# Two adapter layers in Winograd form: where the second down phase keeps its first inputs and its first bias

## The chip, the cores and the metric

The kernel runs on one core of a Trainium2 chip. The metric is the device time of one execution in microseconds. TensorE multiplies, ScalarE, VectorE and GpSimd do the elementwise work, and SyncE issues nearly all DMA transfers. Everything is float32.

## What is computed

There are two layers with the same form. Each of 128 samples (128 rows of 1024 numbers) has a role, one of three, and each role has weights of its own. A layer goes down to 512 numbers, through a Gelu, up to 1024, adds its input, and normalises:

```python
def _L0_cond_ref(role, hidden_states, W_down, b_down, W_up, b_up, gamma, beta):
    h = jnp.einsum('bsh,bhk->bsk', hidden_states, W_down[role]) + b_down[role][:, None, :]
    h = jax.nn.gelu(h, approximate=False)
    u = jnp.einsum('bsk,bkh->bsh', h, W_up[role]) + b_up[role][:, None, :]
    y = hidden_states + u
    mean = jnp.mean(y, axis=-1, keepdims=True)
    var = jnp.mean(jnp.square(y - mean), axis=-1, keepdims=True)
    yn = (y - mean) * jax.lax.rsqrt(var + LN_EPS)
    return yn * gamma[role][:, None, :] + beta[role][:, None, :]
...
    x = _L0_cond_ref(itok_B_1_2, x, L0_cond_W_down, L0_cond_b_down, L0_cond_W_up, L0_cond_b_up, L0_cond_gamma, L0_cond_beta)
    x = _L1_cond_ref(itok_B_1_2, x, L1_cond_W_down, L1_cond_b_down, L1_cond_W_up, L1_cond_b_up, L1_cond_ln_w, L1_cond_ln_b)
```

## The kernel before

**Pairs and places.** On the chip the kernel sorts the samples by role and forms 63 pairs of two samples of one role, and one left-over pair whose samples may differ. The roles are put in order of frequency; a role's position in that order is its *place*, 0 to 2. The first 21 pairs (`NFIRST`) are surely of place 0, so they need only place 0 of the weights and the biases. For the other pairs the place is read into a register.

**Phases.** The work is four phases: down and up of layer 0, down and up of layer 1. Each runs over all 64 pairs in one `sequence`, in which the left-over pair stands in the middle; so the last up pairs of a phase have the numbers 60, 61 and 62. Between the phases the results go through DRAM: `hd` holds what a down phase gives, `mid` what the up phase of layer 0 gives.

**One pair.** A pair is multiplied in Strassen-Winograd form: seven products of quarter size (`item_products`, s1 to s7 at L444 to L472), with four sums of the input quarters made by GpSimd (`winograd_sums`, L401 to L404) and four sums of weight quarters made beforehand. The products gather in three kinds of PSUM banks, b, a and e. Banks b and e begin with a copy of the bias by ScalarE (`seeded`, L428), the *seed*; a product can't begin before its seed. Between two products into the same bank the bank is read: in a down pair by ScalarE (L549, L557) or VectorE (L553), in an up pair by VectorE (L618, L627).

A `Down` pair loads x in eight transfers of 128 KB (`quartered`, L387), four for each sample; VectorE turns each sample with one block transpose (L525, the *turn*); then GpSimd's sums and the products follow. It ends with Gelus on ScalarE (L554, L557) and a store of h to `hd` (L562). An `Up` pair loads h and x (L584, L590), turns h (L596), and ends with the norm: ScalarE takes mean and squares (L689 to L694), GpSimd the inverse root (L695), VectorE scales (L698), and the last factor and beta come from ScalarE and GpSimd for one sample (L705, L706) and from VectorE for the other (L708). Then the result is stored to `mid` (L710).

**Buffers.** The tag q has four buffers of 128 x 1024. The two x of a down pair lie in it (`xqd`), and so do the two outputs of an up pair (`ou`), from L693 to their store. In the up phase q holds outputs alone; near its end it holds x of the first down pairs too. A buffer is given out in the order of the requests and is taken only when its last user is done. The tag t has three buffers, for x of an up pair or the turned x of a down pair.

**Weights.** `wall` holds eight slots; a weight block is one slot with three places of 1024 columns each. Seven blocks, named as in `ORDER`, serve a phase, and the eighth slot is free for the next phase's first block, B11. The others are loaded into the slots of the finished phase as its last products end (L813): place 0 first, places 1 and 2 over the next pairs, block by block. So the blocks of the coming phase have two unused places for some time.

**Order.** The order is written out by hand. A pair has a `base` time, in slots, 7 slots to a pair, and each step is put at a time relative to it with `at(time, step)`; the heap `events` runs the steps in order of time, and L849 to L860 keep that order on each engine. SyncE's queue is in order as well: an issue that waits holds all behind it. Eight semaphores serve the DMAs in turn, so that a transfer is issued only when the one eight before it has landed.

**Around the change.** For the first three down pairs of layer 1, `go` (which turns both samples, starts the sums and plans the products) stands at base - 7.2 (L768), the loads of x at base - 11.9 and - 11.8 (L756). The biases of that phase are loaded at L790 to L800: place 0 into table 0 just after the last up pair has begun, places 1 and 2 some pairs later, and all three once more into table 2 in the middle of the phase, since the next up phase needs table 0. The bias' right half has its left half subtracted by VectorE (L133). The first down pair has its first seed at base - 0.6 (L744) and the others at base - 4.

Of the kernel before, what the change touches and what calls it, by code (L numbers as in the profile page):

```python
# [10 lines left out]
F32 = mybir.dt.float32  # L11
I32 = mybir.dt.int32
AF = mybir.ActivationFunctionType
ALU = mybir.AluOpType
ENG = mybir.EngineType
# [4 lines left out]
P = 128  # L20
SQ = 32
NQ = P // SQ
# [4 lines left out]
def kernel(  # L27
# [57 lines left out]
    def flat(tag, bufs, name, size=2048):  # L85
        return work.tile([P, size], F32, tag=tag, name=name, bufs=bufs)
# [416 lines left out]
    class Down:  # L503
# [5 lines left out]
            self.tag = f"d{layer}_{n}"  # L509

        def load(self):
            self.xq = [
                flat("q", 4, f"xq{self.tag}_{s}", H).rearrange("p (a c) -> p a c", a=NQ)
                for s in range(2)
            ]
            self.srcs = x_of(self.layer, self.n, ENG.SP)
            quartered(self.xq[0:1], self.srcs[0:1])

        def load_rest(self):
            quartered(self.xq[1:2], self.srcs[1:2])  # L520

        def prepare(self):
            self.a = flat("t", 3, "xT" + self.tag).rearrange("p (s j c) -> p s j c", s=2, c=P)
            for s in range(2):
                nc.vector.transpose(  # L525
                    self.a[:, s].rearrange("p j (t a) -> p j a t", t=SQ),
                    self.xq[s].rearrange("p a (i j) -> p j a i", i=SQ),
                )
                if s == 0 and self.early:
                    first_sum("T1", 0)  # L530
            self.sums = None
            if self.n < NPAIR:
                self.sums = flat("s", 3, "S" + self.tag, 1792)[:, 0:1536].rearrange(
                    "p (m j c) -> p m j c", m=3, c=P
                )
                winograd_sums(self.sums, self.a, nc.vector if self.early else nc.gpsimd)
            set_places(self, [ENG.PE, ENG.Activation])
# [185 lines left out]
    def at(time, step):  # L723
        heapq.heappush(events, (time, next(count_), step))
# [7 lines left out]
    for k, ph in enumerate(phases):  # L732
        for m, n in enumerate(sequence):
            base = SLOTS * (k * NI + m)
            box = {}
            kind = Up if ph.up else Down

            def load(box=box, ph=ph, n=n, kind=kind, m=m):
                item = box["item"] = kind(ph, n)
                item.m = m  # L740
                item.early = ph is phases[0] and m == 0
                item.last = ph is phases[-1] and m == NI - 1
                if ph is phases[2] and m == 0:
                    item.SEED = -0.6  # L744
                if m == left_over_at + 1:
                    item.SEED = -1.65
                item.load()


            if ph.up:  # L750
                first, rest = (-16 if m < 3 else -11.5), -7
            elif k == 0:
                first = {0: -30, 1: -19, 2: -19, 3: -17.4}.get(m, -19)
                rest = -27 if m == 0 else first + 0.05
            else:
                first, rest = -11.9, -11.8  # L756
            at(base + first, load)
            at(base + rest, lambda box=box: box["item"].load_rest())

            def go(box=box, base=base):  # L760
                item = box["item"]
                item.prepare()
                for time, step in item.products() + item.finish():
                    at(base + time, step)


            prepare = {1: 3.5 - base, 2: 8.6 - base}.get(m, kind.PREPARE) if k == 0 else kind.PREPARE
            at(base + (-7.2 if ph is phases[2] and m < 3 else prepare), go)  # L768
        if k + 1 < len(phases):

            nxt = phases[k + 1]
            later_places = lambda time, load: [
                at(base + time + SLOTS * 2 * i, lambda k_=k_: load([k_])) for i, k_ in enumerate(range(1, R))
            ]
            place_0, others = slice(0, 1), slice(1, R)
            if nxt.up:
                at(base - 2 * SLOTS, lambda nxt=nxt: nxt.new_bias(0))
                at(base - 2 * SLOTS, lambda nxt=nxt: nxt.load_bias([0]))
                at(base - 2 * SLOTS + 3, lambda nxt=nxt: nxt.subtract(place_0))
                at(base - 2 * SLOTS + 3, nxt.set_bias)  # L780
                at(base - 2 * SLOTS, lambda nxt=nxt: nxt.load_gamma([0]))
                at(base + 2 * SLOTS - 1, lambda nxt=nxt: nxt.load_beta([0]))
                later_places(6 * SLOTS - 1, nxt.load_gamma)
                later_places(7 * SLOTS - 1, nxt.load_beta)
                later_places(10 * SLOTS - 1, lambda p, nxt=nxt: nxt.load_bias(p))
                at(base + 14 * SLOTS - 1.9, lambda nxt=nxt: nxt.subtract(others))
            else:


                at(base + 1.6, lambda nxt=nxt: nxt.new_bias(0))  # L790
                at(base + 1.6, lambda nxt=nxt: nxt.load_bias([0]))
                at(base + 4.2, lambda nxt=nxt: nxt.subtract(place_0))
                at(base + 4.2, nxt.set_bias)
                later_places(5 * SLOTS - 0.6, lambda p, nxt=nxt: nxt.load_bias(p))
                at(base + 10 * SLOTS - 1.9, lambda nxt=nxt: nxt.subtract(others))
                half = base + SLOTS * NI // 2
                at(half, lambda nxt=nxt: nxt.new_bias(2))
                at(half, lambda nxt=nxt: nxt.load_bias())
                at(half + SLOTS, lambda nxt=nxt: nxt.subtract())
                at(half + SLOTS, nxt.set_bias)  # L800

            if k == 0:
                places = [(7, -SLOTS), (5, 4), (4, 6), (0, 8), (1, 8), (2, 10), (3, 10)]
                spare = 6
            else:
                slots = [spare] + [ph.weights[name].slot for name in ORDER]
                places = [(slot, 2 * i - 2) for i, slot in enumerate(slots[:-1])]
                places[0], spare = (slots[0], -SLOTS), slots[-1]
            for name, (slot, free) in zip(ORDER, places):
                nxt.weights[name] = block = Block(slot)  # L810

                def load_part(k, to=block, src=scratch[nxt.layer, nxt.up][name]):
                    nc.sync.dma_start(to.v[:, k], src[:, k])  # L813


                at(base + free + 0.75, lambda f=load_part: f(0))
                for k_ in range(1, R):
                    later_on = SLOTS * (1 + ORDER.index(name)) + 3.5 * k_
                    at(base + later_on + 0.75, lambda f=load_part, k_=k_: f(k_))
# [70 lines left out]
```

## Time and profile before

| | |
|---|---|
| median of 3 runs | 3151.09 us (3149.3 to 3152.04) |
| the profiled execution | 3151.07 us |
| its span, first to last instruction | 3149.3 us |
| TensorE matmul busy | 3112.8 us, 99% of the span |
| VectorE | 1976.1 us, 63% |
| GpSimd | 1793.0 us, 57% |
| ScalarE | 1201.7 us, 38% |
| mean granted TensorE clock | 0.996 |
| DMA | 642.74 MB, mean 204 GB/s |

All times inside the profile count from the first instruction of the one execution that was profiled. A row of a timeline gives start, duration, engine, line, operation, what is written and read, how many instructions are merged, and in brackets how long the engine stood idle before it and what ended that. "SPq" rows are issues of transfers by SyncE. Names are the program's, without numbers: `xqd` and `xTd` are x of a down pair as loaded and as turned, `Sd` its sums; `xu`, `hTu`, `ou` are x, turned h and output of an up pair; `bu`, `au`, `eu`, `bd`, `ad`, `ed` are the PSUM banks of up and down pairs. An up product is recorded as four matmuls of 128x512 and a down product as eight of 128x256. The hand-over from the up phase of layer 0 to the down phase of layer 1 lies between 1550 and 1615 us.

### The profile page before, as it was taken

How to read it: one execution, taken by the hardware profiler on the slowest of the kernel's cores; microseconds unless marked ns; L12 is line 12 of the kernel's file. 1: busy time of each engine (PE TensorE's matmuls, PEld its weight loads, DVE VectorE, ACT ScalarE, POOL GpSimd, SP SyncE). 2: the span in 40 equal slices, each digit the busy share in tenths (PEclk: the TensorE clock that was granted, in tenths of full speed). 3: DMA queues.
4: the chain of work that ended last, by engine and by line, in shares of the span. 5: the costliest groups of instructions: out<-in, count | busy, mean ns of one | idle time of the engine just before them, and what ended most of it. 6: DMA issues, size and time to landing. Idle time of an engine off the chain costs nothing. (4 is left out here: it accounts for less than half of the span.)

```text
span 3149.3 us, 42330 instructions
## 1 busy us (share of the span) xinstructions
PE 3112.8 (99%) x10806; PEld 2056.5 (65%) x10806; DVE 1976.1 (63%) x2795; ACT 1201.7 (38%) x2814; POOL 1793.0 (57%) x1396
## 2 busy tenths in 40 slices
PE   8999999999999999999999999999999999999998
PEld 6888888888544444444478888888884444444443
DVE  5555454544678777877754444444437777777777
ACT  1222222222355545454432222222224545554554
POOL 3454444454577767777654443343436777677776
PEclk9999999999999999999999999999999999999999
DMA  7878888886886666666696555555568766666665
GB/s 189 209 208 215 208 209 205 217 210 191 284 288 214 225 213 221 215 219 220 220 252 163 129 134 138 131 129 133 130 180 294 265 217 218 219 215 223 214 226 173
DMA packets 430454, 642.74 MB, mean 204 GB/s; under 512 B 36113, under 2 KB 305938, under 8 KB 429074
## 3 DMA queue, kind: packets, MB, share of 16 engines
q1 hardware_dynamic: 429746, 638.47, 68.9%
q8 instruction: 102, 1.67, 0.2%
q10 hardware_dynamic: 480, 1.57, 0.2%
q14 instruction: 126, 1.03, 0.1%
HBM read 405.54 MB, written 234.36 MB: 203 GB/s over the span
## 5 line engine op out<-in xcount | busy, mean ns | idle before, releaser
L410 PE MATMUL bu<-wall,hTu 128*128 (+1 forms) x2048 | 924.1, 593 | 6.1 <-DVE xu L618 5.5
L525 DVE STREAM_TRANSPOSE xTd<-xqd 128x1024 f32<-128x1024 f32 x256 | 518.2, 2088 | 354.4 <-PE bd L410 275.1
L410 PEld LDWEIGHTS bu<-wall,hTu 128*128 128x128 f32 x2048 | 389.9, 190 | 495.8 <-issue 458.7
L401 POOL TENSOR_TENSOR Sd<-xTd 128x512 f32<-128x512 f32 x125 | 161.0, 1288 | 799.9 <-DVE xTd L525 799.9
L695 POOL TENSOR_TENSOR varu<-varu,mhalf 128x1 f32<-128x1 f32 x254 | 334.9, 1319 | 394.5 <-ACT varu L694 394.5
L410 PE MATMUL bd<-wall,xTd 128*128 (+1 forms) x2080 | 492.2, 380 | 4.0 <-ACT bd L428 4.0
L410 PE MATMUL eu<-wall,hTu 128*128 (+1 forms) x1040 | 488.0, 592 | 0.0
L410 PE MATMUL bd<-wall,Sd 128*128 (+1 forms) x2016 | 476.3, 379 | 0.8 <-ACT hd L549 0.8
L698 DVE SCALAR_TENSOR_TENSOR ou<-xu,meanu,tables 128x1024 f32<-128x1024 f32 x254 | 326.3, 1285 | 224.8 <-ACT ou L693 224.5
L410 PEld LDWEIGHTS bd<-wall,xTd 128*128 128x128 f32 x2080 | 396.2, 191 | 60.1 <-ACT bd L428 4.8
L410 PEld LDWEIGHTS bd<-wall,Sd 128*128 128x128 f32 x2016 | 383.0, 190 | 54.5 <-issue 2.6
L554 ACT ACTIVATE hd<-hd 128x256 f32<-128x256 f32 x382 | 158.8, 416 | 533.5 <-DVE hd L553 533.4
L410 PEld LDWEIGHTS eu<-wall,hTu 128*128 128x128 f32 x1040 | 197.6, 190 | 247.5 <-issue 224.8
L689 ACT ACTIVATE partu<-statu 128x2 f32<-128x2 f32 x254 | 51.6, 203 | 732.4 <-DVE xu L627 732.4
L706 POOL TENSOR_TENSOR ou<-ou,tables 128x1024 f32<-128x1024 f32 x127 | 299.4, 2357 | 0.0
L693 ACT ACTIVATE ou<-xu,meanu 128x1024 f32<-128x1024 f32 x254 | 291.7, 1148 | 13.5 <-DMA mid<-ou 4.9
L410 PE MATMUL ed<-wall,xTd 128*128 (+1 forms) x1072 | 254.6, 381 | 3.0 <-DVE xTd L402 3.0
L401 POOL TENSOR_TENSOR hTu<-hTu 128x256 f32<-128x256 f32 x126 | 203.2, 1613 | 65.9 <-DVE hTu L596 51.7
L410 PE MATMUL ad<-wall,xTd 128*128 (+1 forms) x1008 | 238.2, 379 | 0.0
L410 PE MATMUL ed<-wall,Sd 128*128 (+1 forms) x1008 | 238.1, 379 | 0.0
L410 PE MATMUL au<-wall,hTu 128*128 (+1 forms) x504 | 236.8, 592 | 0.0
L410 PEld LDWEIGHTS ed<-wall,xTd 128*128 128x128 f32 x1072 | 204.5, 191 | 31.9 <-issue 3.6
(110 smaller groups left out, 3329.5 us busy)
## 6 DMA issues: line engine op xcount, KB each, us to landing
xqd<-in_x_dram SPq DMA_DIRECT2D x512, 128.0 KB, 3.3
hd<-hd SPq DMA_DIRECT2D x256, 256.0 KB, 2.4
xu<-in_x_dram SPq DMA_DIRECT2D x128, 512.0 KB, 4.8
mid<-ou SPq DMA_DIRECT2D x128, 512.0 KB, 6.0
xqd<-mid SPq DMA_DIRECT2D x512, 128.0 KB, 3.9
xu<-mid SPq DMA_DIRECT2D x128, 512.0 KB, 5.8
out_dram<-ou SPq DMA_DIRECT2D x126, 512.0 KB, 5.7
hqu<-hd SPq DMA_DIRECT2D x244, 256.0 KB, 6.4
```

What stands on the lines that cost most here:

```text
L401: engine.tensor_tensor(dst[:, 1], a11, a21, ALU.subtract)
L410: nc.tensor.matmul(ps[:, 0:cols], a[:, j], w.rhs(r, j, cols), start=start and j == 0, stop=j == n - 1, skip_group_check=True,)
L525: nc.vector.transpose(self.a[:, s].rearrange("p j (t a) -> p j a t", t=SQ), self.xq[s].rearrange("p a (i j) -> p j a i", i=SQ),)
L554: nc.scalar.activation(y, y, AF.Gelu)
L689: nc.scalar.mul(part, self.stat[:, s], -1.0 / H)
L693: nc.scalar.activation(box["o"], self.x[:, s], AF.Square, bias=m, accum_out=v)
L695: nc.gpsimd.tensor_tensor(v, v, mhalf[:, 0:1], ALU.pow)
L698: nc.vector.scalar_tensor_tensor(box["o"], self.x[:, s], box["m"][:, 0:1], row(self.ph.gamma), ALU.add, ALU.mult)
L706: nc.gpsimd.tensor_tensor(o, o, row(self.ph.beta), ALU.add)
```

## The change

Four things are changed, all of them at that hand-over.

The x of the first three down pairs of layer 1 isn't loaded into q. It goes into places 1 and 2 of the weight blocks B11, B21 and T2 of the coming phase, which aren't loaded yet. The load for the first of these pairs stands at base - 15 in place of - 11.9.

For these three pairs the two turns are separate steps: the first sample's at base - 7.2, the second's with the sums at base - 5.

The first bias (place 0) has a tile of its own, `first_bias`, loaded four pairs before the last up pair and subtracted one pair later; the first down pair's seed stands at base - 4 as the others'. It serves until the twelfth down pair.

All three rows are loaded into table 2 as the eighth, ninth and tenth down pair begin, and used after their subtraction 1.9 slots ahead of the twelfth. The loads of places 1 and 2 into table 0, and those in the middle of the phase, are gone.

```diff
@@ class Down
         def load(self):
-            self.xq = [
-                flat("q", 4, f"xq{self.tag}_{s}", H).rearrange("p (a c) -> p a c", a=NQ)
-                for s in range(2)
-            ]
+            if self.among_weights:
+                block = self.ph.weights[ORDER[self.m]].v
+                self.xq = [block[:, 1 + s] for s in range(2)]
+            else:
+                self.xq = [flat("q", 4, f"xq{self.tag}_{s}", H) for s in range(2)]
+            self.xq = [t.rearrange("p (a c) -> p a c", a=NQ) for t in self.xq]
...
+        def turn(self, s):
+            nc.vector.transpose(
+                self.a[:, s].rearrange("p j (t a) -> p j a t", t=SQ),
+                self.xq[s].rearrange("p a (i j) -> p j a i", i=SQ),
+            )
+
+        def begin_turns(self):
+            self.a = flat("t", 3, "xT" + self.tag).rearrange("p (s j c) -> p s j c", s=2, c=P)
+            self.turn(0)
+
         def prepare(self):
-            self.a = flat("t", 3, "xT" + self.tag).rearrange("p (s j c) -> p s j c", s=2, c=P)
-            for s in range(2):
-                nc.vector.transpose(
-                    self.a[:, s].rearrange("p j (t a) -> p j a t", t=SQ),
-                    self.xq[s].rearrange("p a (i j) -> p j a i", i=SQ),
-                )
-                if s == 0 and self.early:
-                    first_sum("T1", 0)
+            if not self.among_weights:
+                self.begin_turns()
+            if self.early:
+                first_sum("T1", 0)
+            self.turn(1)
@@ the pairs' steps
-                if ph is phases[2] and m == 0:
-                    item.SEED = -0.6
+                item.among_weights = ph is phases[2] and m < 3
...
-                first, rest = -11.9, -11.8
+                first = -15 if m == 0 else -11.9
+                rest = first + 0.1
...
-            at(base + (-7.2 if ph is phases[2] and m < 3 else prepare), go)
+            if ph is phases[2] and m < 3:
+                at(base - 7.2, lambda box=box: box["item"].begin_turns())
+                prepare = -5
+            at(base + prepare, go)
@@ the biases of the second down phase
-                at(base + 1.6, lambda nxt=nxt: nxt.new_bias(0))
-                at(base + 1.6, lambda nxt=nxt: nxt.load_bias([0]))
-                at(base + 4.2, lambda nxt=nxt: nxt.subtract(place_0))
-                at(base + 4.2, nxt.set_bias)
-                later_places(5 * SLOTS - 0.6, lambda p, nxt=nxt: nxt.load_bias(p))
-                at(base + 10 * SLOTS - 1.9, lambda nxt=nxt: nxt.subtract(others))
-                half = base + SLOTS * NI // 2
-                at(half, lambda nxt=nxt: nxt.new_bias(2))
-                at(half, lambda nxt=nxt: nxt.load_bias())
-                at(half + SLOTS, lambda nxt=nxt: nxt.subtract())
-                at(half + SLOTS, nxt.set_bias)
+                def first_bias(nxt=nxt):
+                    nxt.bias = row = const.tile([P, 1, K], F32, name="first_bias")
+                    r = reg(role_of, 0, [ENG.SP], R - 1)
+                    nc.sync.dma_start(row[:, 0], nxt.vectors[0][ds(r, 1), :].to_broadcast((P, K)))
+
+                def subtract_first(nxt=nxt):
+                    left, right = nxt.bias[:, :, 0 : K // 2], nxt.bias[:, :, K // 2 :]
+                    nc.vector.tensor_tensor(right, right, left, ALU.subtract)
+
+                at(base - 4 * SLOTS + 0.6, first_bias)
+                at(base - 3 * SLOTS + 0.6, subtract_first)
+                at(base + 8 * SLOTS - 0.6, lambda nxt=nxt: nxt.new_bias(2))
+                for k_ in range(R):
+                    at(base + (8 + k_) * SLOTS - 0.6, lambda k_=k_, nxt=nxt: nxt.load_bias([k_]))
+                at(base + 12 * SLOTS - 1.9, lambda nxt=nxt: nxt.subtract())
+                at(base + 12 * SLOTS - 1.9, nxt.set_bias)
```

Here `base` in the last part is that of the last up pair.

## The prediction

> **What bounds the kernel now.** I read the page first: TensorE is busy for 99% of the span, at the full clock in all 40 slices, so nearly all of the time is a gapless run of matmuls and a change can gain only where that run is broken. Next I asked who TensorE waits for, in the stretch where the up phase of layer 0 hands over to the down phase of layer 1:
>
> ```profile
> PE bu L410 <- DVE xu L618: 5.5, 1, 5.5
> PE bd L410 <- ACT bd L428: 4.0, 1, 4.0
> PE bd L410 <- ACT hd L549: 0.8, 1, 0.8
> ```
>
> Columns: total us, times, longest. Three waits. The timeline of TensorE shows what they cost (start, us, what):
>
> ```profile
> 1559.49 1.88 PE L410 MATMUL au<-wall,hTu 128*128 x4
> 1561.20 1.88 PE L410 MATMUL eu<-wall,hTu 128*128 x4
> 1568.58 6.00 PE L410 MATMUL bu<-wall,hTu 128*128 x8 [5.50 <-DVE xu L618]
> 1574.42 1.88 PE L410 MATMUL eu<-wall,hTu 128*128 x4
> 1580.27 3.58 PE L410 MATMUL bd<-wall,xTd 128*128 128x256 f32 x8 [3.97 <-ACT bd L428]
> 1611.28 1.89 PE L410 MATMUL ed<-wall,Sd 128*128 128x256 f32 x8
> 1614.01 1.97 PE L410 MATMUL bd<-wall,Sd 128*128 128x256 f32 x8 [0.84 <-ACT hd L549]
> ```
>
> An up product (4 records) starts 1.716 us after the one before, a down product (8 records) 1.726. From 1562.92 (1561.20 + 1.716, where the stalled product was due) to 1614.01 stand 6 up and 15 down products, 10.30 + 25.89 = 36.19 us of work in 51.09 us: 14.9 us are lost. They are 5.66 idle and 2.41 of slow matmuls (5.84 for two products instead of 3.43), 4.13 idle and 1.68 slow (3.41 instead of 1.73), and 1.0 at the third.
>
> Then the engines behind them. The first two rows are ScalarE, then VectorE, then SyncE:
>
> ```profile
> 1561.28 1.15 ACT L693 ACTIVATE ou<-xu,meanu 128x1024 f32<-128x1024 f32 x1 [4.93 <-DMA mid<-ou]
> 1579.85 0.36 ACT L428 COPY bd<-tables 128x256 f32<-128x256 f32 x1
> 1562.56 1.28 DVE L698 SCALAR_TENSOR_TENSOR ou<-xu,meanu,tables 128x1024 f32<-128x1024 f32 x1 [5.61 <-ACT ou L693]
> 1563.88 4.01 DVE L525 STREAM_TRANSPOSE xTd<-xqd 128x1024 f32<-128x1024 f32 x2
> 1567.79 0.64 DVE L618 TENSOR_TENSOR xu<-bu,xu 128x512 f32<-128x512 f32 x1
> 1575.55 0.43 DVE L133 TENSOR_TENSOR tables<-tables 128x256 f32<-128x256 f32 x1 [2.49 <-DMA tables<-in_L_cond_b_down_dram]
> 1552.64 0.36 SPq L710 DMA_DIRECT2D mid<-ou  x1
> 1553.05 8.48 SPq L387 DMA_DIRECT2D xqd<-mid  x8
> 1571.29 0.34 SPq L122 DMA_DIRECT2D tables<-in_L_cond_b_down_dram  x1
> ```
>
> Gap one: L693 of the up pair 60 has its mean at 1556.36, but its output needs one of the four buffers of tag q, two of which hold x of down pair 0; so it waits for the store issued at 1552.64. VectorE works in order: L698, both turns (4.01), and only then L618, which frees TensorE. L618's own product was ready at 1557.77. Gap two: the first bias is fetched at 1571.29, VectorE stands 2.49 us for it, and ScalarE copies the seed at 1579.85, behind two norms.
>
> **The Trainium skill.** "TensorE: Matmul & The Clock Gate", What's actually happening: after an idle window of about 3.4 us the array runs at half clock for about as long. The trace agrees: slow matmuls follow the 5.5 and 4.0 us gaps, none follows the 0.84 one (1.97 against 1.89). "Perfetto Trace Analysis", Optimization Strategy: gaps on the engine that should be full can mean missing room for the next tile. It speaks of repeated gaps; here there is one, but its end is a released buffer (4.93 on mid<-ou). "DMA: Bandwidth & Descriptors", Rules for kernel authors: issue early, wait late. Here a 512 KB store that finds the queue empty lands in 2.61 us (issued 1537.72), the one at 1552.64 in 8.57. "GPSIMD Engine Reference", Key points: GpSimd and VectorE contend in some forms; L708 took 2.33 us at 1601.56 beside GpSimd's sums, 1.33 at 1586.22.
>
> **The change, part by part.** The order of instructions on TensorE and GpSimd is the same in both builds.
> *x out of tag q.* L693 of pair 60 then takes a buffer stored long before: it starts at 1556.38 (0.32 after its mean began, as for the pair before: 1544.04 to 1544.36). L698 follows at 1557.66 (+1.28), the first turn at 1558.98 (+1.32, as 1562.56 to 1563.88).
> *One turn instead of two ahead of L618.* L618 starts 1.95 later (half of 3.91), 1560.93, and TensorE can go on at 1561.72 (+0.79, as 1567.79 to 1568.58), before 1562.92. Gap one goes: 8.1 us. With both turns it would be 1563.67, a 0.75 us gap; so moving x does most of it and splitting the turns the rest. The second turn comes behind L708, at 1563.44 to 1565.45; GpSimd's four sums take 6.1 us from there (1568.03 to 1574.15 before), and the third, which down pair 0 needs at 1574.96, is done by 1570.3. Cover: 4.6 us.
> *x loaded earlier.* Eight issues go in ahead of the store at 1549.69, where SyncE is idle from 1541.65. By the built order each waits for the transfer eight before it; the last of those lands at 1547.49, so the last issue is near 1547.8 and the store isn't held. x lands by about 1552.5 (0.6 us each), needed at 1558.98. Cost 0; x of pair 62 behind it (landed 1556.82) has 4 us to spare.
> *Bias in its own tile.* The load goes to about 1528, its subtraction (0.43) to about 1535.6, in the steady up phase. It delays hq of pair 60 (landed 1535.65, used 1536.27) by 0.5 to 1.4 us. L618 has over 3 us before TensorE needs it there, so I take 0; bounds 0 and 1 us. The seed stands right behind the eu seed, about 1559.4. TensorE reaches down pair 0 at 1568.07 and doesn't wait (its B11 block landed at 1558.93): 5.8 us more.
> *Later biases.* Two rows less to load and 512 columns less to subtract, off the path: 0. All three are loaded as the eighth to tenth down pair begin and first used after the subtraction ahead of the twelfth: 0.
>
> **What is late next.** The norms of the last two up pairs, ScalarE and VectorE in turn, now lie beside a TensorE that is some 12 us ahead. By the same distances: L698 of pair 61 at 1568.62 and 1572.39; turn 1573.71; L708 1576.27; turn 1577.6; L553 1579.55; L554 1580.0; the seed of down pair 1 ends at 1580.69. TensorE needs it at 1580.13: 0.6 us. Then L549 of pair 0 stands behind the norm of pair 62 and ends at 1583.1 (needed 1582.5): 0.7. The next L549 1586.87 (needed 1586.65): 0.3. The seed of pair 2 waits for the second L553, behind L708 and a turn: ends 1594.6 to 1595.6 as L708 takes 1.3 or 2.3 (needed 1593.9): 0.8 to 1.8. The store of hd, which holds TensorE at 1614.01 now, moves with L708 of pair 62 (1603.88 now, 1591.1 to 1592.2 then) and lets TensorE go at 1601.3 to 1602.3, needed about 1602: 0 to 0.3.
> Weight blocks: T2 is issued when the first x transfer of pair 1 has landed, about 1568.5, and lands about 1574.0 (needed 1574.96). B22 lands 1585.2 to 1586.5 (needed 1586.65), T4 1590 to 1591.3 (needed 1590.4). So 0 to 1.5 us, taken as 0.1.
> Residue 0.6 + 0.7 + 0.3 + 1.3 + 0.1 = 3.0 us, bounds 1 and 8; all too short for a clock dip. Gain 14.9 - 3.0 = 11.9 us. After that nothing hands it back: turns of pair 3 are done about 1603, TensorE's first use is 1607.5.
> Sum against the profiled execution: 3151.07 (span 3149.3 and 1.8 around it) - 11.9 = **3139.2 us**. The median shown, 3151.09, is the same to 0.02.
>
> **Rivals.** *Norms and transfers are a little late* (forecast, 3137.5 to 3141.5): 65%.
> *All of the loss goes* (14.9 us, 3136.2): needs the ladder above to run 0.6 to 1.8 us faster than its rows; against it is that every distance is a measured one. 8%.
> *Transfers take the place of the waits.* From 1585 to 1640 the DMA engines are 0.8 to 1.1 busy, and the same bytes must come 12 us sooner. If T2, B22, T4 and the hd store each come 1 to 2 us late, the residue is 6 to 8: 3142 to 3144.5. For it: eight x transfers (4.7 us) lie ahead of T2 and T4. Against: SyncE's issues move by the same 10 to 12 us, since they follow L708 and L706. 19%.
> *The change doesn't do what it says*: another q buffer or wait holds L693, only gap two goes: 3151.1 - 5.8 = 3145.3. The built order names the older store. 5%.
> *Slower: x is still late, now at the head of VectorE.* The first turn stands ahead of L618; if x of pair 0 lands after 1560.1, each us costs TensorE one, plus 2.4 for the clock. Landing at 1569.7 eats the 11.9; from 1576 it is slower by 0.2% (3157.4). It would take 34 us from issue; the slowest x transfer here took 8.8. 3%.
>
> **From chances to numbers.** About 0.2% (6.3 us) is what a measurement of this kernel can tell from no change. The first three cases lie under 3144.8: faster 0.92. The fourth and a third of the last lie within 0.2%: 0.06. The rest of the last is slower: 0.02. The range runs from full removal to the middle of the transfer case: 3136.2 to 3143.6.
>
> **What would show it.** Right: L693 of pair 60 without a wait for mid<-ou; no TensorE wait on L618 and none over 2 us in the seam; eight records of bu in 3.6 us, not 6.0; bd's first seed about 1559; remaining short waits on ACT L428 and L549. Wrong: a wait on wall<-T or wall<-B on TensorE, a wait of the first turn on mid, a clock dip in the seam, or gaps where the bias was put, near 1536.

## The result and the profile after

The changed kernel takes 3144.24 us (median of 12 runs, 3142.03 to 3147.28), the kernel before 3151.49 (12 runs, 3149.05 to 3155.07). The ratio is 0.9977, with a 95% interval from 0.9969 to 0.9984: faster by 7.25 us, between 5.0 and 9.8. The forecast was 3139.2, so 4.7 us of the expected 11.9 are missing, and the time lies above the range that was given, 3136.2 to 3143.6. The profiled execution took 3143.59 us (span 3141.8), at a mean granted clock of 0.998 where it was 0.996.

Who TensorE waits for at the hand-over, after (total us, times, longest):

```profile
PE bd L410 <- ACT hd L560: 1.6, 2, 1.2
PE bd L410 <- DMA wall<-T: 0.8, 1, 0.8
PE bd L410 <- POOL varu L706: 0.7, 1, 0.7
PE bu L410 <- POOL ou L717: 0.7, 1, 0.7
PE bd L410 <- ACT bd L428: 0.5, 1, 0.5
PE bu L410 <- DVE xu L638: 0.4, 1, 0.4
```

Both large waits (5.5 and 4.0) are gone. In their place stand six kinds of short ones. Line numbers have moved: L525 is now L527, L596 L607, L618 L629, L627 L638, L693 L704, L695 L706, L698 L709, L705 L716, L706 L717, L708 L719, L549 L560, L553 L564, L710 L721, L562 L573, L813 L832. So L706 is GpSimd's addition of beta in the kernel before, and its inverse root in the changed one.

Two of these names have to be read with care, since the profile puts a wait for several engines down to the one that came last. The up product at 1564.96 needs its bank read by L629, which ended 0.14 us earlier; L717 ended in between. The down product at 1577.98 needs its bank read by ScalarE's L560, which ended 0.10 us earlier; L706 ended only after the product had begun. TensorE's timeline of the changed kernel:

```profile
1560.66 1.88 PE L410 MATMUL au<-wall,hTu 128*128 x4
...
1564.96 3.67 PE L410 MATMUL bu<-wall,hTu 128*128 x8 [0.70 <-POOL ou L717]
...
1570.19 1.89 PE L410 MATMUL bd<-wall,xTd 128*128 128x256 f32 x8
...
1607.11 1.97 PE L410 MATMUL bd<-wall,Sd 128*128 128x256 f32 x8 [1.24 <-ACT hd L560]
```

The eight records of bu take 3.67 us instead of 6.00, the first ones of bd 1.89 instead of 3.58: no slow matmuls are left. The wait on the store of hd, 0.84 before, is 1.24.

A yardstick follows from these rows. From the start of the last up pair's second product (au, 1560.66) to the third product of down pair 2 (1607.11) stand 8 up and 15 down products, 8 x 1.716 + 15 x 1.726 = 39.62 us of work. I call this stretch the *seam*, and what it takes beyond 39.62 its *loss*. Before: 1614.01 - 1559.49 = 54.52, loss 14.90, as the prediction counted. After: 46.45, loss 6.83. So 8.07 us were gained where 11.9 were forecast, and 3.83 of the seam are missing. Elsewhere the two profiled executions differ too: TensorE's wait at the kernel's start (on L402) is 3.0 us in one and 4.8 in the other, and lies between 2.6 and 6.6 in the profiles of this study. That is why the seam is a sharper measure than the time, and why I compare seams below.

The engines behind TensorE, after (rows of ScalarE, VectorE, SyncE, GpSimd, from the timeline):

```profile
1559.57 1.15 ACT L704 ACTIVATE ou<-xu,meanu 128x1024 f32<-128x1024 f32 x1
1562.61 0.36 ACT L428 COPY bd<-first_bias 128x256 f32<-128x256 f32 x1
1606.59 0.37 ACT L560 COPY hd<-bd 128x256 f32<-128x256 f32 x1 [7.11 <-DMA hd<-hd]
...
1524.55 2.49 DVE L811 TENSOR_TENSOR first_bias<-first_bias 128x256 f32<-128x256 f32 x1
...
1595.35 0.45 SPq L721 DMA_DIRECT2D mid<-ou  x1
...
1602.68 0.39 SPq L573 DMA_DIRECT2D hd<-hd  x1
...
1524.41 2.34 POOL L717 TENSOR_TENSOR ou<-ou,tables 128x1024 f32<-128x1024 f32 x1
```

L704 of up pair 60 no longer waits for a store, the first seed stands right behind the up pair's, and one turn (1562.17, 2.11 us) lies ahead of L629 (1564.17). That is the mechanism that the prediction described. Two rows don't fit it. The subtraction of the first bias took 2.49 us, where 0.43 was counted; it stands beside L717 of GpSimd, which began 0.14 us earlier, and ends 0.29 us after it (1524.41 + 2.34 = 1526.75, 1524.55 + 2.49 = 1527.04). And SyncE's queue from the last store of mid to the first store of hd got longer: 1602.68 - 1595.35 = 7.33 us, where it was 1609.22 - 1603.91 = 5.31 before.

### The profile page after: what moved, and what is told of

It is laid out like the page before. It is cut to its first block, busy times and chain, and to the rows that moved or that the text cites. A ratio compares the mean times of both kernels' runs of the same rounds, so it can differ in the third digit from the quotient of the medians.

```text
span 3141.8 us, 42319 instructions
## 1 busy us (share of the span) xinstructions
PE 3109.3 (99%) x10806; PEld 2053.3 (65%) x10806; DVE 1977.3 (63%) x2794; ACT 1203.6 (38%) x2814; POOL 1793.9 (57%) x1396
## 4 chain that ended last, share of the span: by engine, by line
PE 48%; DMA 1%; DVE 1%; issue 0%; ACT 0%; DVEq 0%; SPq 0%; ACTq 0%
PE bu L410 14%; PE bd L410 14%; PE eu L410 7%; PE ed L410 7%; PE au L410 3%; PE ad L410 3%; DMA mid<-ou 0%; DVE ou L719 0%; DMA wall<-mid 0%; DMA hd<-hd 0%; ACT ou L704 0%; DVE xu L635 0%; DVE last_stat L636 0%; DVE xu L638 0%; DVEq L905 0%
## 5 line engine op out<-in xcount | busy, mean ns | idle before, releaser
L527 DVE STREAM_TRANSPOSE xTd<-xqd 128x1024 f32<-128x1024 f32 x250 | 505.0, 2087 | 354.1 <-PE bd L410 275.4
L706 POOL TENSOR_TENSOR varu<-varu,mhalf 128x1 f32<-128x1 f32 x254 | 333.7, 1314 | 383.1 <-ACT varu L705 383.1
L709 DVE SCALAR_TENSOR_TENSOR ou<-xu,meanu,tables 128x1024 f32<-128x1024 f32 x254 | 327.1, 1288 | 253.3 <-ACT ou L704 253.0
L717 POOL TENSOR_TENSOR ou<-ou,tables 128x1024 f32<-128x1024 f32 x127 | 299.5, 2358 | 0.1
L704 ACT ACTIVATE ou<-xu,meanu 128x1024 f32<-128x1024 f32 x254 | 292.2, 1150 | 8.3
```

The lines of the kernel that those rows point to most:

```text
L527: nc.vector.transpose(self.a[:, s].rearrange("p j (t a) -> p j a t", t=SQ), self.xq[s].rearrange("p a (i j) -> p j a i", i=SQ),)
L704: nc.scalar.activation(box["o"], self.x[:, s], AF.Square, bias=m, accum_out=v)
L706: nc.gpsimd.tensor_tensor(v, v, mhalf[:, 0:1], ALU.pow)
L709: nc.vector.scalar_tensor_tensor(box["o"], self.x[:, s], box["m"][:, 0:1], row(self.ph.gamma), ALU.add, ALU.mult)
L717: nc.gpsimd.tensor_tensor(o, o, row(self.ph.beta), ALU.add)
```

## The experiments

Each row is one kernel. "Loss" is that of the seam in the one execution that was profiled; "later" adds the eleven products behind it (before: 0.08 us more). Each ratio is to the executions of the kernel before that were made beside it, whose medians lie between 3151.39 and 3152.33 us. Most intervals of the changed kernels overlap, so the times alone don't rank them; what follows rests on the seams and on the waits in them.

| kernel | loss | median us (runs) | ratio to before [95%] |
|---|---|---|---|
| before | 14.90 | 3151.49 (12) | |
| changed | 6.83 | 3144.24 (12) | 0.9977 [0.9969, 0.9984] |
| x alone | 9.35 | 3146.79 (20) | 0.9986 [0.9979, 0.9992] |
| bias alone, subtraction clear | 12.14 | 3148.64 (12) | 0.9988 [0.9979, 0.9996] |
| before, spare subtraction | 15.99 | 3153.75 (20) | 1.0009 [1.0002, 1.0016] |
| changed, subtraction clear | 5.49 | 3143.08 (9) | 0.9974 [0.9964, 0.9984] |
| changed, subtraction 24 pairs early | 5.75 | 3142.69 (10) | 0.9973 [0.9963, 0.9982] |
| clear, turns together | 7.00 | 3144.4 (14) | 0.9977 [0.9969, 0.9985] |
| changed, places later | 5.42 | 3142.23 (6) | 0.9968 [0.9956, 0.998] |
| clear, places later | 3.95 | 3139.54 (5) | 0.9965 [0.9952, 0.9978] |
| the same, subtraction 22 pairs earlier | 4.28 | 3140.51 (5) | 0.9962 [0.9948, 0.9976] |
| clear, store of hd ahead of x | 3.59, later 8.4 | 3144.11 (14) | 0.9977 [0.9969, 0.9984] |
| clear, places later, hd and T4 ahead of x | 3.68, later 5.3 | 3142.05 (6) | 0.9969 [0.9957, 0.9982] |
| clear, places later, second turn later | 6.05 | 3141.86 (7) | 0.9968 [0.9957, 0.998] |

My theory: the two gaps went as forecast, and the missing 3.83 us of the seam have two causes, VectorE's delay by the subtraction and a store of hd held up in SyncE's queue. The rivals: one cause alone, or an error in the forecast's ladder of norms.

**The subtraction clear of GpSimd.** The same step, 4.9 slots (0.7 of a pair) later:

```diff
-                at(base - 3 * SLOTS + 0.6, subtract_first)
+                at(base - 2 * SLOTS - 1.5, subtract_first)
```

> The changed kernel with the subtraction of the first bias half a pair later, where GpSimd is idle, between L638 and the next L629. Seam here means from the start of the last up pair's second product to the third product of down pair 2: 54.5 us before, 46.45 in the changed kernel, 39.6 without any loss. Theory (the subtraction met GpSimd's L717, took 2.49 us instead of 0.43, and VectorE never made the 2 us up): subtraction 0.4 to 0.5 us, L709 of the next pairs with a TensorE wait ahead again, seam 42.5 to 44.5, time about 3 us under the changed kernel. Rival (the rest of the loss is transfers: T4 and the hd store): seam within 1 us of 46.45, time unchanged.

Measured, VectorE's timeline of this kernel:

```profile
1535.09 0.42 DVE L811 TENSOR_TENSOR first_bias<-first_bias 128x256 f32<-128x256 f32 x1
```

With GpSimd idle the subtraction takes 0.42 us, as priced. The waits that the profile puts down to L717 and L706 are gone, and the loss falls by 1.34, to a seam of 45.11: less than the theory's 2 to 4, more than the rival's 1. Part of what the early products gain is given back at the store of hd, which now holds TensorE for 1.87 us beyond the product's time rather than 1.40.

The Trainium skill, "SBUF — State Buffer", SBUF: two separate sides, states the mechanism: a VectorE operation with two inputs in SBUF and a GpSimd operation that reads SBUF need the same pair of ports; whichever starts first has it for its whole length, and the other stands still. The trace agrees: L811 is done 0.29 us after L717.

**The same delay in the kernel before.** A subtraction of a tile that nothing else uses, at the same place:

```diff
+                spare_row = const.tile([P, 1, K], F32, name="spare_row")
+                at(base - 40 * SLOTS - 1.5, lambda: nc.vector.memset(spare_row, 0.0))
+                def subtract_spare():
+                    left, right = spare_row[:, :, 0 : K // 2], spare_row[:, :, K // 2 :]
+                    nc.vector.tensor_tensor(right, right, left, ALU.subtract)
+                at(base - 3 * SLOTS + 0.6, subtract_spare)
```

> The kernel before, with one more subtraction of 128x256 on a spare tile at the place where the changed kernel subtracts the first bias; nothing else. Theory: it takes about 2.5 us beside L706, VectorE stays some 2 us behind to the end of the phase, and the seam grows from 54.5 to about 56.5; 2 us slower than before. Rival (a lag of VectorE is made up within a pair or two, as the waits on TensorE of 0.4 to 0.85 us in each pair suggest): seam 54.5, time as before.

Measured, TensorE's timeline:

```profile
1571.20 6.05 PE L410 MATMUL bu<-wall,hTu 128*128 x8 [7.43 <-DVE xu L618]
```

The spare subtraction, at 1524.05, takes 2.49 us again, and 47 us later the first gap is 7.43 us instead of 5.50. The product behind the store of hd, 1.00 us late before, is 0.09 late now; that takes part of it up, so that the loss grows by 1.09 and not by the theory's 2. So a delay of VectorE in the steady up phase is still there at the hand-over, in the kernel before as in the changed one, and without the bias' own transfer.

**Why it isn't made good.** Take the lag from TensorE's start of an up pair's au product to VectorE's end of reading it: 3.81 us in the steady phase. In the changed kernel it is 5.95, 5.91 and 5.87 in the pairs after the subtraction. VectorE and ScalarE wait for each other in the norms, twice in a pair, as here in the changed kernel:

```profile
1533.13 1.28 DVE L709 SCALAR_TENSOR_TENSOR ou<-xu,meanu,tables 128x1024 f32<-128x1024 f32 x1 [1.27 <-ACT ou L704]
...
1545.10 1.28 DVE L709 SCALAR_TENSOR_TENSOR ou<-xu,meanu,tables 128x1024 f32<-128x1024 f32 x1 [1.27 <-ACT ou L704]
```

That is one round in 11.97 us; TensorE's pair is 7 x 1.716 = 12.01. So 0.04 to 0.05 us a pair are regained, and 2.1 us need some 45 pairs. To see it, the subtraction was put far ahead and left in collision:

```diff
-                at(base - 4 * SLOTS + 0.6, first_bias)
-                at(base - 3 * SLOTS + 0.6, subtract_first)
+                at(base - 25 * SLOTS + 0.6, first_bias)
+                at(base - 24 * SLOTS + 0.6, subtract_first)
```

> The changed kernel with load and subtraction of the first bias 21 pairs earlier, at the same place inside a pair, so that it meets GpSimd again. Theory: VectorE's loop of 11.98 us against TensorE's 12.02 gives back 0.04 us a pair, so 0.8 us in 20 pairs; 1.2 us or more of lag are left, seam 44.5 to 46.5. Rival (a lag goes within a few pairs, and it counts only close to the seam): like the kernel with the subtraction moved clear of GpSimd, 42.5 to 44.5 or what that one shows.

Measured: at 1270.99 the subtraction takes 2.49 us as well. The lag starts at 5.95 and falls by 0.05 a pair to 4.84 before the last pair; it isn't gone "within a few pairs". The loss of 5.75 alone would not tell that from the rival, since it is only 0.26 above that with the subtraction clear: the early products still lose 0.80 us where that kernel loses 0.06, but the store of hd, which comes at its own time, takes less (1.46 for 1.87).

**The weights' places later.** Places 1 and 2 of the coming blocks are loaded four pairs later; the subtraction is clear:

```diff
-                    later_on = SLOTS * (1 + ORDER.index(name)) + 3.5 * k_
+                    later_on = SLOTS * ((5 if k == 1 else 1) + ORDER.index(name)) + 3.5 * k_
```

> The kernel with the clear subtraction, and the loads of places 1 and 2 of the phase's weight blocks four pairs later (first used at the twenty-second pair). What is left of the loss there is 5.5 us (seam 45.1 against 39.6), 1.0 of it ahead of the product that needs T4 and 1.9 ahead of the one that waits for the store of h. Theory (transfers crowd the seam): without B11's places 1 and 2 in the queue the second store to mid lands in 4 to 5 us instead of 7.4, the eighth x transfer of pair 3 and the store of h behind it go out 2 us sooner, and the wait on ACT L560 falls from 1.7 to under 0.5; seam 43 to 44. Rival (the norms of the last up pairs on ScalarE and VectorE set it all): seam 45.1 within 0.3.

Measured, TensorE's waits at the hand-over, and SyncE's timeline:

```profile
PE bd L410 <- ACT bd L428: 1.1, 2, 0.6
PE bu L410 <- DVE xu L638: 0.4, 1, 0.4
PE bd L410 <- ACT hd L560: 0.3, 1, 0.3
PE bd L410 <- POOL varu L706: 0.3, 1, 0.3
```

```profile
1591.11 1.40 SPq L721 DMA_DIRECT2D mid<-ou  x2
...
1597.62 1.34 SPq L573 DMA_DIRECT2D hd<-hd  x2
```

In the changed kernel the last store of mid comes 0.81 us behind a load of 512 KB for a place of block B, and lands after 6.61 us; before, it came 4.01 us behind that load and landed after 3.06. The eighth transfer of x behind it has to wait for its semaphore and is issued at 1601.97, just after the store's landing at 1601.96; the store of hd stands behind that transfer. Without the place loads the distance from the store of mid (1592.20) to the store of hd is 5.42 us, near the 5.31 of before, and TensorE doesn't wait for it. The seam is 43.57, as the theory had it, and the loss 3.95 us. That the time, 3139.54, is near the forecast for the change is chance: this is another kernel, and its loss is 0.95 over the forecast's 3.0.

**The same with the collision.** Only that line is changed in the changed kernel.

> The changed kernel with places 1 and 2 of the weight blocks loaded four pairs later, and nothing else changed: the subtraction of the first bias stays where it meets GpSimd (2.49 us). Seam 46.45 in the changed kernel, 43.57 with the places later and the subtraction clear, 45.11 with the subtraction clear alone. Theory, the two causes add: VectorE's lag of 2.1 us comes through by as much as it did beside the early places (1.34) or a little more, since nothing later absorbs it: seam 44.9 to 45.6, 3140.9 to 3141.6 us. Rival, the places were the whole cause and the collision only shifts where the loss is seen: seam 43.6, 3139.5 us.

Measured, two rows of TensorE's timeline:

```profile
1568.40 3.67 PE L410 MATMUL bu<-wall,hTu 128*128 x8 [0.79 <-POOL ou L717]
1581.40 1.97 PE L410 MATMUL bd<-wall,Sd 128*128 128x256 f32 x8 [0.72 <-POOL varu L706]
```

The first wait is back (the product comes 0.96 us late, 0 with the subtraction clear), the second is longer (0.72 for 0.26), and there is none on the store of hd. The loss of 5.42 (seam 45.04) lies where the theory of two causes put it, the time 0.6 us above. So the loss in four kernels is: 6.83 as changed, 5.49 with the subtraction clear, 5.42 with the places later, 3.95 with both. Each cause is worth 1.3 to 1.5 us, whether the other is there or not. That rules out one cause alone. Together the two are 2.88 of the 3.83 us.

**Both parts of the change alone.** First x alone: the biases and the first seed stay as before.

> The kernel before with only x of three pairs in the weight blocks and the turns apart; bias as before. By the prediction's ladder gap one goes (8.1 us). The bias load stands behind the store of pair 60, is issued about 1564 and lands about 1568.5; the seed stands behind both norms of pair 61, ends about 1573 where TensorE needs it at 1568.1: a gap of 5 us and 1.7 us of slow clock stay. They also give the later steps time, so that most of the residue hides: seam 47 to 48.5. Rival (the two gaps are independent, as the prediction counted them): seam 46.45 + 5.8 = 52.3, or 51 with the subtraction clear.

Measured, TensorE's timeline:

```profile
1576.84 3.78 PE L410 MATMUL bd<-wall,xTd 128*128 128x256 f32 x8 [7.25 <-ACT bd L428]
```

Then the bias alone, with the subtraction clear; x stays in tag q.

> The kernel before with one part of the change alone: the first bias in a tile of its own, with its subtraction half a slot late enough to be clear of GpSimd, the seed beside the others, and the later biases as the change has them. x of the first three pairs stays in tag q, with both turns together. Seam (start of the last up pair's second product to the third product of down pair 2) 39.62 us without loss, 54.52 before, 48.97 with x alone. Theory, the two gaps are independent: gap one (8.1 us) stays, gap two (5.8) goes, and most of the residue stays hidden behind gap one's delay; seam 48.7, about 3145.6 us. Theory, parts overlap (with x alone 5.55 of seam were gained rather than 8.1, and the bias then added only 2.5 or 3.9): the bias alone gains more than what it adds last, 5 to 6 us of seam. Rival: the seed of the first pair still waits, for the norms of pairs 61 and 62 stand ahead of it on ScalarE; then the gain is 2.5 us or less, seam 52.

Measured, two of TensorE's waits:

```profile
PE bu L410 <- DVE xu L618: 6.3, 1, 6.3
PE bd L410 <- DVE hd L553: 1.4, 1, 1.4
```

x alone removes gap one, but TensorE then waits 7.25 us for the bias instead of 3.97, so it gains 5.55 us; the seam, 48.97, is 0.5 above the theory's range and far from the rival's independent gaps. The bias alone removes gap two (5.8) and gains 2.76, since gap one costs 0.5 more (VectorE comes into it 0.76 us further behind, see below) and reads of the down pairs come late behind it. Neither of the two theories held for the bias alone: its 2.76 is near the rival's 2.5, but not by the rival's mechanism, for the first seed doesn't wait. Together (subtraction clear) they gain 9.41, 1.10 more than their sum.

**The turns together.** Subtraction clear, both turns ahead of L629, one edit: `prepare = -7.2` for `-5`.

> The changed kernel with the clear subtraction, and both turns of each of the three pairs together at base - 7.2 again. By the prediction's ladder L618 of the last pair starts 2 us later: a TensorE gap of about 0.75 us ahead of its third product, while the later steps stand as they did; seam 0.7 to 2 us above that of the clear subtraction. Rival (splitting is worth nothing, since the second turn stands ahead of other late steps): the same seam within 0.3 us, or a shorter one.

The loss is 7.00, 1.51 more than with the turns apart. TensorE's up product waits for L629 and comes 0.94 us late, where the prediction had worked out 0.75; the rest comes at later reads.

**The store of hd ahead of x.** Subtraction clear; the loads of x of down pair 3 stand behind the first store of hd.

```diff
+            if ph is phases[2] and m == 3:
+                first, rest = -10.25, -10.15
```

> The kernel with the clear subtraction, and x of down pair 3 loaded behind the first store of h instead of ahead of it. Theory: that store stands behind eight x transfers, of which the last waits for a landing; ahead of them it goes out about 1598 + 3.1 of shift instead of 5 us later, TensorE's wait on ACT L560 (1.7) goes, seam 43.2 to 43.6. Rival (the store is late because DMA engines are full, not because of its place): seam 44.5 or more. A loss is possible at pair 3, whose x comes 2 to 3 us later with about 6 us to spare.

Measured, TensorE's longest wait, and VectorE's timeline:

```profile
PE bd L410 <- DVE hd L564: 2.9, 1, 2.9
```

```profile
1608.31 2.07 DVE L527 STREAM_TRANSPOSE xTd<-xqd 128x1024 f32<-128x1024 f32 x1 [1.34 <-DMA xqd<-mid]
```

The wait moves rather than goes: x of pair 3 is now late (VectorE stood 6.71 us for the first turn and 1.34 for the second), its turns hold L564, and the loss in the eleven products after the seam is 4.8 us. With the places later, and T4 issued between the two halves of x of pair 2 (`rest = -10.2`), the same happens in small:

> Both of the former edits, and T4 issued between the two halves of x of down pair 2 instead of behind them. Theory: the wait for T4 (0.9) goes as well, seam 42 to 43, which is what the prediction's ladder gave (42.5); time about 2.5 us under the kernel with the clear subtraction alone. Rival: seam 44 or more.

The seam, 43.30, lies between theory and rival, and with the later products the loss is 5.3, more than the 3.95 of the plain order with the places later. So another order in SyncE's queue moved the wait; fewer transfers in it removed one. T4 is on time here, but the seed of down pair 2 behind it comes 0.97 us late.

**The second turn later.** Places later, subtraction clear, `prepare = -3.9` for `-5`: the second turn behind the reads that free TensorE.

> Places later and subtraction clear as in the run that gave 3139.54 us and a seam of 43.57, and the second turn of the first three down pairs 1.1 slots later (base - 3.9 for base - 5), so that it stands behind the reads of PSUM that TensorE waits for rather than ahead of them; the orders of ScalarE, TensorE and GpSimd are the same, only VectorE's is changed. Theory: what is left of the loss (3.9 us) is VectorE's order at the hand-over, as the prediction's ladder has it; the waits on L638, L428 and L560 shrink, seam 42 to 42.8, time about 1 us less than 3139.5. Rival: GpSimd's sums start 2 us later behind the later turn and TensorE waits for them at the third product, or the waits only move to the Gelus; seam 43.6 or more, no gain.

Measured, rows of GpSimd, ScalarE and TensorE:

```profile
1576.58 2.35 POOL L404 TENSOR_TENSOR Sd<-xTd,Sd 128x512 f32<-128x512 f32 x1
1579.48 1.15 ACT L716 ACTIVATE ou<-ou,varu 128x1024 f32<-128x1024 f32 x1 [2.68 <-POOL varu L706]
1580.98 3.50 PE L410 MATMUL bd<-wall,Sd 128*128 128x256 f32 x8 [2.07 <-ACT hd L560]
```

The rival was right that nothing is gained. GpSimd's sums start later with the turn, L404 meets VectorE (2.35 us instead of 1.27), the inverse root L706 stands behind it (1578.89), L716 behind L706, and the read L560 behind L716. The loss is 6.05 us; the reads that were to come free (L638, the seed) did, and the wait moved to the chain behind GpSimd. Not all of the 2.10 us more is the turn's: a transfer of h came 0.97 us late at 1480.95 in this execution, and VectorE entered the hand-over 0.56 us further behind than in the kernel with 3.95.

**The subtraction clear and early.** As with the places later, but load and subtraction 22 pairs earlier, clear of GpSimd.

> As the run that gave 3139.54 us (places later, subtraction clear of GpSimd), with load and subtraction of the first bias 22 pairs earlier, the subtraction again clear of GpSimd. With it 24 pairs early beside GpSimd VectorE had 1.05 us of its lag of 2.1 still to regain at the hand-over. Theory: a subtraction clear of GpSimd leaves no lag of note, so its place is free: seam 43.3 to 43.7 as in that run (43.57), and 3139 to 3140.5 us again. Rival: the few tenths that VectorE is still behind in that run when the seam begins come from the subtraction, and 22 pairs take them back: seam 42.9 to 43.2. Third: the 3139.54 us stood on five runs and chance; the time is 3141 to 3142 with the same seam.

The loss is 4.28 (seam 43.90, 0.2 above the theory's), the time 3140.51 us; neither rival shows. VectorE's timeline tells why it isn't lower:

```profile
1479.58 1.36 DVE L607 STREAM_TRANSPOSE hTu<-hqu 128x512 f32<-128x512 f32 x2 [1.07 <-DMA hqu<-hd]
```

Long after the subtraction, a transfer of h came late in this execution. The lag, back at 3.81 by then, rose to 5.04, and the loop had brought it down only to 4.74 before the last pair. So a late transfer costs what the collision costs.

The lags before the last up pair put all these kernels in one line. In the eight that keep the changed kernel's order of computing steps at the hand-over, the third product of that pair, the one behind it and the third product of down pair 0 lose together the lag less 4.03 us, to within 0.02:

| kernel | lag | these three lose |
|---|---|---|
| changed, places later | 5.96 | 1.92 |
| changed | 5.87 | 1.86 |
| subtraction 24 pairs early | 4.84 | 0.80 |
| clear and early, places later | 4.74 | 0.71 |
| clear, places later | 4.46 | 0.43 |
| clear, places later, hd and T4 ahead of x | 4.22 | 0.19 |
| clear, store of hd ahead of x | 4.14 | 0.11 |
| clear | 4.08 | 0.06 |

The hand-over forgives 0.22 us over the steady 3.81 and no more. The kernels with the subtraction clear are not at 3.81 because of the bias' load: in each of the seven that load it four pairs ahead with a clear subtraction, VectorE stood 0.15 to 0.70 us for the transfer of h behind it; in the kernel before and in x alone, which load no bias there, it didn't.

Here T4 comes 1.08 us late though the place loads are away, so T4's lateness isn't theirs.

## Why the prediction was wrong in size and right in kind

Its ladder can be set beside the traces, term by term: by how much a product starts later than the one before it allows.

| step of the prediction | forecast us | changed | clear, places later |
|---|---|---|---|
| last up pair, third product, read L629 | 0 | 0.87 | 0 |
| third product of down pair 0, first L560 | 0 | 0.91 | 0.43 |
| last up pair, read L638 | 0 | 0.62 | 0.64 |
| seed of down pair 1 | 0.6 | 0.64 | 0.64 |
| L560 behind the norm of pair 62 | 0.7 | 0.59 | 0.59 |
| the next L560 | 0.3 | 0.26 | 0.26 |
| seed of down pair 2 | 1.3 | below 0.1 | 0.80 |
| weight blocks | 0.1 | 1.00 | 0.12 |
| store of hd | 0 | 1.40 | 0 |
| the rest, mostly the products behind these waits, each under 0.12 | 0 | 0.54 | 0.47 |
| sum | 3.0 | 6.83 | 3.95 |

- *Gap one goes, gap two goes*: right. Both are gone whole, slow matmuls too, and the split of the turns is worth what was said (0.75 worked out, 0.94 measured).
- *"Bias in its own tile ... L618 has over 3 us before TensorE needs it there, so I take 0; bounds 0 and 1 us"*: this step failed first. The price 0.43 came from a row where GpSimd was idle; beside L717 it is 2.49. The prediction had named such collisions for L708 and didn't ask what GpSimd does at the subtraction's new place. The profile before shows it, at the very time that the prediction gave, 1535.6:

```profile
1535.35 2.35 POOL L706 TENSOR_TENSOR ou<-ou,tables 128x1024 f32<-128x1024 f32 x1
```

(That time is one pair too late: load and subtraction stand at 1517.79 and 1524.55. The place inside the pair is the same, and so is the neighbour.) And the cover was misread: TensorE indeed didn't wait there, but 3 us of time before a deadline isn't slack in a loop that has 0.04 us of it a pair. The lag was carried three pairs on, to where only 0.22 us are free; neither these 3 us nor the "cover: 4.6 us" of the third down product, which priced GpSimd's sums but not the read L560 behind a norm, were there. The early products lost 1.86 us. With the subtraction clear they lose 0.06, but the store of hd then takes 0.47 more, so the collision cost 1.3 us in all, and 1.5 where that store isn't late. The bias' load, which the prediction said would delay h and took at 0, is a further 0.4 of the 3.95.
- *"Against: SyncE's issues move by the same 10 to 12 us"*: this failed second. The issues that follow the norms move; the place loads were not followed, and the distance from the last store of mid to the store of hd grew from 5.31 to 7.33. The step "hd store 0 to 0.3" measured 1.40. So the rival *transfers take the place of the waits* holds for this part: 1.4 us of its 3 to 5, in one of the four transfers it named. The wait on `wall<-T`, which the prediction had named as a sign of being wrong, came too, but costs little (see T4 below). The rival's time, 3142 to 3144.5, fits the median for a reason that is half another one.
- *What is late next, 3.0 us*: the named terms held within 0.11 us for three of four. One was missed (the read L638 behind the first turn of pair 1, 0.6), and so was the short delay of each product behind a wait (0.5 in all); one came out smaller (the seed of pair 2). With both causes away the sum is 3.95 to 4.28, about 1 us over the forecast.
- *T4 and the seed of pair 2* stand two products apart and cover each other: 1.00 and below 0.1 in the changed kernel, 0.12 and 0.80 with clear and later places, 1.08 and 0 with the subtraction early as well, 0 and 0.97 with T4 ahead of x. In the eight kernels of the table of lags the sum is 0.9 to 1.1, where the forecast had 1.4 (1.3 and 0.1), so T4's lateness is none of the excess.
- *Left open*: why T4 is late in one execution and not in another. It hangs on when the store of pair 61 and B22's load are issued; I haven't separated it. And 8.07 us of seam against 7.25 us of time is within the interval of the ratio.

The version with the subtraction clear of GpSimd and the places four pairs later has the lowest times of all: 3139.54 and, with the subtraction early, 3140.51 us, against 3144.24 of the changed kernel. The intervals of the ratios overlap a little; that the seam is 2.9 us shorter, and by which waits, the traces show.

## What to carry to other kernels

Before an instruction is priced at a row of the profile, look at what the engine that shares its ports does at the new place, and take the row from there. "Not needed for 3 us" covers a delay only if the loop behind it is faster than the bound engine by enough to win it back; compare the period of the two, and follow the lag to the place where the order of work changes. When a change brings stores and loads forward, list the transfers that are tied to other events and stay, for they will stand in the same queue.

## What the runs showed of the hardware that was not expected

- The collision is whole, not shared: 0.42 us became 2.49, alike in four kernels, and the later instruction ended 0.27 to 0.29 us after the earlier one. A longer one is held too: L709 at 1571.65 took 2.16 us instead of 1.28, having started 0.19 behind GpSimd's L403. It works in the other direction as well: L404, which started 0.07 us behind L709 in the kernel with the later turn, took 2.35 instead of 1.27.
- A gap shorter than the one that the prediction cited slows the clock: in the kernel with the later turn TensorE's matmuls stood idle for 2.07 us, its weight loads for 2.87, and the next eight records took 3.50 us instead of 1.97. The windows of this stretch (columns: length; busy time and count of PE, PEld, DVE, ACT, POOL; granted clock; DMA share; GB/s):

```profile
1578.50:1580.90 2.40, 0.41 (x1) 0.00 (x0) 2.40 (x4) 1.42 (x3) 1.66 (x4) 1.00 0.43 172
1580.90:1582.60 1.70, 1.62 (x5) 1.32 (x6) 1.70 (x5) 0.84 (x3) 1.70 (x1) 0.60 0.02 5
```

The clock falls from 1.00 to 0.60, and in the next 1.7 us to 0.50. The same kernel's gap of 1.72 us is followed by no dip (1.97). "TensorE: Matmul & The Clock Gate", What's actually happening, gives an idle window of about 3.4 us; here the measurement decides, and a gap of 2.07 us was enough.
